# Cross-attention block: batch 0's second MLP product by seven block products, and the order of work around it

## The chip, the cores and the metric

The kernel runs on one core of a Trainium2 chip. A core has TensorE (matrix products into PSUM, with a separate weight load that runs beside them), VectorE, ScalarE and GpSimd (elementwise work), SyncE, whose queue (SP) issues most DMAs, and DMA engines. The metric is the device time of one execution in microseconds (us), the median of several runs. All data are float32; one matmul of this type leaves two records in the trace.

## The reference

Four batches; 512 rows of width 512; 16 heads of width 32; an inner width of 2048.

```python
x = layer_norm(hidden_states, ln1_w, ln1_b)
q, k, v = x @ q_w + q_b, enc @ k_w + k_b, enc @ v_w + v_b      # split into 16 heads
attn = softmax(where(mask, q @ k.T / sqrt(32), min))
hidden = (attn @ v) @ cproj_w + cproj_b + hidden_states
y = gelu(layer_norm(hidden, ln2_w, ln2_b) @ fc_w + fc_b)       # inner width 2048
return hidden + (y @ proj_w + proj_b)
```

## The kernel before

**Attention.** The work is cut into 16 units (4 batches x 4 groups of four heads) and each unit into two halves of 256 query rows: 32 blocks p = 0 to 31, written out one after the other. Every engine takes its instructions in the written order. A block begins with the attention product of an earlier half (`attend`, L401, tile `av`; from block 10 on that of half p-2), then computes eight score tiles (`scores`, L312), one in each of the eight PSUM banks. VectorE adds the mask and finds the minimum (`soften`, L319), ScalarE takes the exponential, VectorE transposes in 32x32 tiles into `tb` (`turn`, L331; the last transpose is L360). The blocks of `tb` are then exchanged between partition quarters into `pT`, `gt` or `xe` (`copies`, L385): four copies by GpSimd and twelve DMAs issued on SP. For half p into `pT` that can start only when the half before it in `pT` has been attended; from half 24 on `xe` takes turns with `pT`, and an exchange is issued at the end of its own block.

**Fills.** Other TensorE work is placed by hand between these steps: `put(p, ...)` (L1104) lists for block p the K, Q and V products of later units (`prep_k` L250, `prep_q` L260, `prep_v_pair` L288), the output product (`cproj` L451) and the next MLP items (`some(n)`, L1073). A block takes them in three places: fill(0) after the eighth score (not if the first item is an fc pair), fill(1) after the transposes, fill(2) at the end. The first two stop at a budget of one chain (`CHAIN`), and the exchange of the block is written between fill(1) and fill(2). Items of cost 0 are VectorE, GpSimd or DMA work.

**MLP in the blocks.** `products` (L571) lists in order what of batches 0 and 1 (`SPLIT`) runs in the blocks: fc pairs c (two columns of 128 of the inner width, seven products of half size, `fc_seven` L634) and proj quarters q (512 of the inner 2048). The activations of a quarter lie in `gT[q % 2]`, so the fc pairs of quarter q overwrite those of quarter q-2. A proj quarter is four items, one for each 128 rows: four 128x512 matmuls into one bank (`proj` L701), and one VectorE addition to the residual `hid`.

**Weights.** fc and proj weights go through a ring of eight entries of 256 KB in `pbt` (`load_mlp`, L582). The entry of a weight is reloaded, on SP and in list order, as soon as the item that uses it last (`last_use`) has been written. For the seven products of an fc pair GpSimd forms sums of its raw weights (`fc_sums`, L679), at the start of a block, for pairs at most two ahead of those computed:

```python
while count[3] < len(fc_pairs) and count[3] < count[4] + 2:
    b, c = fc_pairs[count[3]]
    if ("fcw", b, 2 * c + 1) not in S:
        return
```

Here `count[3]` counts pairs with sums, `count[4]` computed pairs. The weights of K and Q of a unit lie in `ptt`, two entries each, loaded two units ahead. After the blocks come the tail (rest of batch 1's first half of proj, `cproj` of batch 3) and `last_mlps` (L737), which the change touches only in where two tiles lie.

Of the kernel before, what the change touches and what calls it, by code (L numbers as in the profile page):

```python
# [35 lines left out]
IN_G = (1, 3, 5, 7)  # L36
IN_XE = (25, 27, 29, 31)

BY_ROW = ((1, 1), (1, 3))
# [12 lines left out]
def xattn_block(ctx: ExitStack, tc: tile.TileContext, x, rawT, encT, mask, q_w, k_w, v_w, c_w, fc_w, p_w, vecs, rows, out):  # L52
# [5 lines left out]

    const, keep, hids, tiles, small = pools(ctx, const=1, keep=1, hids=4, tiles=4, small=4)
    dram = ctx.enter_context(tc.tile_pool(name="dram", bufs=1, space=bass.MemoryType.DRAM))  # L60
# [28 lines left out]
    ys = const.tile([P, 3, 2, L // 2], F32, tag="ys", name="ys")  # L89
    wsum = const.tile([P, 2, 3, 2, P], F32, tag="wsum", name="wsum")  # L90

    def k_q(w, i):
# [117 lines left out]
    def load_rn(b):  # L210
        S["rows", b] = [hids.tile([P, L], F32, tag="hid2", bufs=2, name=f"rn_{b}_{i}") for i in range(2)]
        for i in range(2):
            nc.sync.dma_start(out=S["rows", b][i], in_=S["rn", b][i : i + 1, :].broadcast_to([P, L]))
# [26 lines left out]
    def load_w(w, queue=None, names=("wk", "wq", "wv")):  # L240
# [4 lines left out]
        for i, (n, src) in enumerate((("wk", k_w), ("wq", q_w), ("wv", v_w))):  # L245
            if n in names:
                S[n, w] = kqv_w(w, i)
                (queue or Q[0]).dma_start(out=S[n, w], in_=src[:, g, :, :])

    def prep_k(w):  # L250
        b, g = divmod(w, NG)
        kT = k_q(w, 0)
        acc = acc_tile(f"acck_{w}")
        for d in range(ND):
            nc.tensor.matmul(acc, S["wk", w][:, d, :], eT[:, d, :], start=(d == 0), stop=(d == ND - 1))  # L255
        load_w(w + 2, names=("wk",))
        nc.scalar.activation(kT, acc, AF.Identity, bias=vec[:, KB + g : KB + g + 1], scale=1.0)
        S["kT", w] = kT

    def prep_q(w):  # L260
        b, g = divmod(w, NG)
        qT = k_q(w, 1)
        parts = [slice(0, L)] if w else [slice(0, 2 * P), slice(2 * P, L)]
        for c in parts:
            acc = acc_tile(f"accq_{w}_{c.start}")[:, c]
            for d in range(ND):
                nc.tensor.matmul(acc, S["wq", w][:, d, :], xT[:, d, c], start=(d == 0), stop=(d == ND - 1))  # L267
            nc.scalar.activation(qT[:, c], acc, AF.Identity, bias=qb[:, g : g + 1], scale=-scale)
        load_w(w + 2, names=("wq",))
        S["qT", w] = qT  # L270
# [16 lines left out]

    def prep_v_pair(w):  # L288
        pair = range(w, w + 2)
# [13 lines left out]
        for u in pair:  # L303
            load_w(u + 2, names=("wv",))
            v_bias(u)

# [121 lines left out]
    def stays(b, t):  # L428

        return b == 0 or b == SPLIT and t < 2  # L430

    def load_h(b, *ts_):

        if ("xa", b) not in S:
            S["xa", b] = dram.tile([L, D], F32, tag=f"xa{b}", name=f"xa{b}")
        for t in ts_:
            if b == B - 1:

                S["h", b, t] = k_q(t // 2, t % 2)
            else:  # L440
                pool, tag, n = (tiles, "xn", 4) if not stays(b, t) else (hids, "hid2", 2) if b else (hids, "hid", 4)
                S["h", b, t] = pool.tile([P, D], F32, tag=tag, bufs=n, name=f"h_{b}_{t}")
# [93 lines left out]
    def load_hid(b, ts_):  # L536

        for t in ts_:
            if ("hid", b, t) not in S:
                S["hid", b, t] = hids.tile([P, D], F32, tag="hid", name=f"hid_{b}_{t}")  # L540
# [41 lines left out]
    def load_mlp():  # L582

        while count[0] < len(weights) and (count[0] < MW or weights[count[0] - MW][3] < count[1]):
# [4 lines left out]
            Q[0].dma_start(out=w, in_=fc_w[:, f, :, :] if name == "fc" else p_w[ts(f, P), :])  # L589
            S[name + "w", b, f] = w  # L590
            count[0] += 1
# [108 lines left out]

    def proj(b, q, t):  # L701
        gelus(q % 2)
        acc = acc_tile(f"accp_{b}_{q}_{t}")
        for k in range(FQ):
            nc.tensor.matmul(  # L705
                acc, gT[q % 2][:, k, ts(t, P)], S["pw", b, q * FQ + k], start=(k == 0), stop=(k == FQ - 1)
            )
        h = S["hid", b, t]
        nc.vector.tensor_tensor(h, acc, h, ALU.add)
        if q == NQ - 1:  # L710
            (nc.gpsimd if b == 0 else nc.sync).dma_start(out=out[b, ts(t, P), :], in_=h)
        count[1] += 1
        load_mlp()

# [22 lines left out]
    def last_mlps():  # L737
# [197 lines left out]
        for b, pairs, new in (  # L935
# [45 lines left out]
            if b == SPLIT:  # L981
                S["more"] = [hids.tile([P, D], F32, tag="hid2", bufs=2, name=f"more_{n}") for n in range(2)]
                S["more"] = [m.rearrange("p (c n) -> p c n", c=NP // 2) for m in (*S["more"], row[:, 2, :])]
                to_split.extend(w_sums(5, pt[:, 2]))
# [19 lines left out]

    def V(w):
        return [(CHAIN, lambda: prep_v_pair(w))]

# [65 lines left out]
    def some(n):  # L1073
# [5 lines left out]
        return taken  # L1079

    def hid_(b, *ts_):
        return do(lambda: load_hid(b, ts_))
# [21 lines left out]
    def put(p, *work, before=(), mid=()):  # L1104
# [52 lines left out]
    put(24, [q15], cb(2), V(14), do(lambda: y_sums(SPLIT)))  # L1157
    put(25, c[:3])
    put(26, c[3:], do(lambda: attend(12, 0)), some(2))
    put(27, some(3))  # L1160
    put(28, some(3))
    put(29, some(4))
    put(30, some(3), hid_(1, 2, 3))
    put(31, some(3))

    due = {p: (p - 2,) for p in range(10, 2 * NW)}
    due |= {p: (p - 3,) for p in range(3, 9)} | {9: (6,), 26: ()}
    for p in range(2 * NW):
# [6 lines left out]
        if p > 10:  # L1175
            fc_sums()

        def fill(n, work=fills[p]):
# [70 lines left out]
```

## Time and profile before

| | us |
|---|---|
| median of 3 runs | 762.18 (762.09 to 762.71) |
| profiled execution, time | 760.67 |
| its span, first to last instruction | 758.9 |
| TensorE busy | 753.9 |
| VectorE busy | 613.4 |
| ScalarE busy | 337.6 |
| GpSimd busy | 339.7 |

The blocks 11 to 31, which hold the MLP items, lie between 161.7 and 487.4 us of the span, the tail and the last MLPs after them. The granted TensorE clock was 0.999 of full speed. In the lines of the profile PE is TensorE, PEld its weight load, DVE VectorE, ACT ScalarE, POOL GpSimd, and SPq the issuing of DMAs by SyncE. A line of a timeline gives the start in us from the start of the span, the length in us, the engine, the line of the kernel, the operation, the tile written and the tiles read, and how many instructions are merged; in brackets stands the idle time just before it and what ended that. A line of a group gives the total busy time in us, the mean of one instruction in ns, and the idle time before. `hid`, `h` and `xa` are the residual rows, `wsum` the sums of fc weights, `pbt` holds the ring, `ptt` the K, Q and V weights and the exponentials.

### The profile page before, as it was taken

To read this page: it belongs to the slowest core of one execution; us is meant where nothing else is said; L and a number is where in the kernel's file an instruction comes from. 1 tells how busy PE (TensorE), PEld (TensorE's weight loads), DVE (VectorE), ACT (ScalarE), POOL (GpSimd) and SP (SyncE) were. 2 spreads that over 40 slices of the span, in tenths; PEclk is the share of its full clock that TensorE was granted. 3 is DMA by queue.
4 is the path that set the end of the run, shared out by engine and by line. 5 is a ranking of instruction groups with operands and counts; after the bars stand their busy time and mean duration, and the time that the engine had idled before them with its cause. 6 is when DMAs were issued, how large, how long until landed. Compare 5 with 4: busy or idle time off the path is not lost.

```text
span 758.9 us, 13040 instructions
## 1 busy us (share of the span) xinstructions
PE 753.9 (99%) x4418; PEld 517.8 (68%) x4418; DVE 613.4 (81%) x1222; ACT 337.6 (44%) x768; POOL 339.7 (45%) x352
## 2 busy tenths in 40 slices
PE   9999999999999999999999999999999999999998
PEld 6655555567574545475454566468888899988997
DVE  3889999879995777887887989949877986956865
ACT  2566766565873574647753567501302221022200
POOL 1549447368664873244575444432050004403153
PEclk9999999999999999999999999999999999999999
DMA  9989889467897776665756867776724402046001
GB/s 329 341 255 247 207 207 257 104 199 200 220 243 229 223 231 177 184 175 129 177 133 186 214 194 193 172 227 215 260 98 135 167 26 91 30 146 214 1 15 43
DMA packets 60577, 134.59 MB, mean 177 GB/s; under 512 B 11312, under 2 KB 17072, under 8 KB 60384
## 3 DMA queue, kind: packets, MB, share of 16 engines
q1 hardware_dynamic: 58448, 126.73, 58.4%
q0 software_dynamic: 1920, 7.01, 2.7%
q8 instruction: 35, 0.57, 0.3%
q14 instruction: 30, 0.25, 0.1%
q10 hardware_dynamic: 144, 0.02, 0.0%
HBM read 69.23 MB, written 11.02 MB: 106 GB/s over the span
## 4 chain that ended last, share of the span: by engine, by line
PE 99%; POOL 0%; issue 0%; DVE 0%; DVEq 0%; POOLq 0%
PE q L646 26%; PE accp L705 11%; PE r L792 10%; PE sc L317 8%; PE av L415 8%; PE acck L255 8%; PE accq L267 8%; PE accc L455 6%; PE accv L278 5%; PE accv L298 3%; PE q1p L853 2%; PE tp L166 1%; PE warm L1044 1%; PE q3p L835 0%; PE q5p L835 0%; PE q4p L835 0%
## 5 line engine op out<-in xcount | busy, mean ns | idle before, releaser
L327 ACT ACTIVATE ptt<-ptt,mn 128x512 f32<-128x512 f32 x256 | 181.7, 711 | 142.8 <-DVE mn L323 142.8
L323 DVE CUSTOM_DVE_ANT_0 ptt<-sc,mb 128x512 f32<-128x512 f32 x256 | 160.6, 682 | 19.9 <-PE sc L317 19.8
L335 DVE STREAM_TRANSPOSE tb<-ptt 128x1024 f32<-128x1024 f32 x128 | 153.3, 1217 | 0.0
L393 POOL COPY pT<-tb 32x1088 f32<-32x1088 f32 x96 | 104.5, 1089 | 83.5 <-DVE oT L420 34.6
L705 PE MATMUL accp<-pbt,gt 128*128 128x512 f32 x192 | 85.3, 596 | 0.0
L646 PE MATMUL q<-yT,gt 128*128 128x256 f32 x320 | 78.9, 379 | 0.0
L667 ACT ACTIVATE ga<-ga,vec 128x512 f32<-128x512 f32 x40 | 26.7, 714 | 93.3 <-DVE ga L600 93.3
L646 PEld LDWEIGHTS q<-yT,gt 128*128 128x128 f32 x320 | 60.8, 190 | 8.1
L705 PEld LDWEIGHTS accp<-pbt,gt 128*128 128x128 f32 x192 | 35.9, 190 | 44.6 <-issue 39.1
L317 PE MATMUL sc<-pbt 32*128 32x512 f32 x512 | 64.7, 614 | 0.0
L646 PE MATMUL q<-ys,gt 128*128 128x256 f32 x240 | 61.6, 379 | 0.0
L255 PE MATMUL acck<-xe,ptt 128*128 128x512 f32 x128 | 59.0, 604 | 0.0
L267 PE MATMUL accq<-xe,ptt 128*128 128x512 f32 (+1 forms) x136 | 58.4, 575 | 0.0
L646 PEld LDWEIGHTS q<-ys,gt 128*128 128x128 f32 x240 | 45.7, 190 | 6.1
L600 DVE TENSOR_TENSOR ga<-q,ga 128x512 f32<-128x512 f32 (+1 forms) x60 | 36.2, 603 | 16.3 <-PE q L646 13.5
L327 ACT ACTIVATION_READ_ACCUMULATOR ptt<-ptt,mn 128x1 f32 x256 | 47.8, 187 | 0.0
L415 PE MATMUL av<-pT,v 128*32 128x256 f32 x768 | 46.4, 382 | 0.0
L267 PEld LDWEIGHTS accq<-xe,ptt 128*128 128x128 f32 x136 | 24.9, 190 | 31.4 <-issue 22.8
L255 PEld LDWEIGHTS acck<-xe,ptt 128*128 128x128 f32 x128 | 23.8, 193 | 30.8 <-issue 24.0
L317 PEld LDWEIGHTS sc<-pbt 32*128 32x128 f32 x512 | 26.9, 184 | 24.8 <-issue 16.9
L455 PE MATMUL accc<-wc,oT 128*128 128x512 f32 x96 | 42.5, 598 | 0.0
L278 PEld LDWEIGHTS accv<-ptt,xe 128*128 128x128 f32 x320 | 37.0, 192 | 4.9 <-DVE mn L323 2.7
(231 smaller groups left out, 1270.4 us busy)
## 6 DMA issues: line engine op xcount, KB each, us to landing
pT<-tb SPq DMA_DIRECT2D x288, 136.0 KB, 2.4
pbt<-p_w_dram SPq DMA_DIRECT2D x40, 256.0 KB, 3.3
gt<-ws SPq DMA_DIRECT2D x20, 512.0 KB, 3.3
gt<-tb SPq DMA_DIRECT2D x48, 136.0 KB, 3.8
xe<-tb SPq DMA_DIRECT2D x48, 136.0 KB, 2.5
pbt<-fc_w_dram SPq DMA_DIRECT2D x24, 256.0 KB, 4.7
gt<-fc_w_dram SPq DMA_DIRECT2D x20, 256.0 KB, 3.3
ptt<-k_w_dram SPq DMA_DIRECT2D x16, 256.0 KB, 4.2
```

The lines of the kernel that those rows point to most:

```text
L255: nc.tensor.matmul(acc, S["wk", w][:, d, :], eT[:, d, :], start=(d == 0), stop=(d == ND - 1))
L267: nc.tensor.matmul(acc, S["wq", w][:, d, :], xT[:, d, c], start=(d == 0), stop=(d == ND - 1))
L317: nc.tensor.matmul(S["sc", w, qt][h], qT[r, ts(qt, P)], kT[r, :], start=True, stop=True)
L323: nc.vector.tensor_tensor_reduce(out=s, in0=S["sc", w, qt][h], in1=S["mb", w // NG], scale=1.0, scalar=FMAX, op0=ALU.add, op1=ALU.min, acc ...
L327: nc.scalar.activation(s, s, AF.Exp, bias=mn, scale=-1.0, accum_out=S["sums", w][:, qt, h : h + 1])
L335: nc.vector.transpose(tv[:, qt % 2, 2 * k : 2 * k + 2], S["ps", w, qt, k])
L393: nc.gpsimd.tensor_copy(pT[ts(i, HD), i], tb[ts(i, HD), i])
L415: nc.tensor.matmul(av[ts(h, HD), : 2 * P].rearrange(shape, **kw), v[:, t, ts(h, HD)], p[t][h], start=(t == 0), stop=(t == NT - 1),)
L455: nc.tensor.matmul(acc, S["oT", b][:, g, ts(t, P)], wc[:, g, :], start=(g == 0), stop=(g == NG - 1))
L646: nc.tensor.matmul(o, x[:, k], y[:, k], start=(k == 0), stop=(k == 1))
L705: nc.tensor.matmul(acc, gT[q % 2][:, k, ts(t, P)], S["pw", b, q * FQ + k], start=(k == 0), stop=(k == FQ - 1))
L792: nc.tensor.matmul(r, x[:, c], w[:, c], start=(c == 0), stop=(c == NP // 2 - 1))
```

## The change

Each proj quarter of batch 0 is computed by seven products of half size in each direction (x11 ... of activations and weights, with sums and differences on both sides) instead of eight. It becomes three items: part 0 (products q1, q5, q2), part 1 (q7, q6), part 2 (q3, q4). The sums that the first part needs (`proj_sums`, through `pre`) are formed by GpSimd ahead of it, the others by GpSimd in part 0, in place over activations and weights. ScalarE keeps q1 (and q5) in the place of blocks that are no longer needed; VectorE or GpSimd joins the results to the residual (`join`). Quarters in `FOUND1` and `FOUND5` join q1 and q5 directly from PSUM; in `COPIED` (quarter 3) ScalarE copies q3 and q4 and GpSimd joins them. Ring entries of the first two weights of a quarter are free after part 1, the others after part 2. K and Q weights have one entry each from unit 10 on, loaded one unit ahead, which frees the room for the two sum tiles x and y; quarter 3 takes the V weights' room. The fills of blocks 14, 15, 18 to 20, 22, 23 and 25 to 30 are laid out anew, with K and Q of unit 13 exchanged and K of unit 12 moved to block 19. The V biases of units 10 and 11 are held back to the start of the next block. The residual tiles of batches 0 and 1 become fixed tiles `hid4` and `hid2`.

```diff
+SINGLE = 10
+FOUND1, FOUND5, COPIED = ((0, 0),), ((0, 0), (0, 3)), ((0, 3),)
...
     def kqv_w(w, i):
-        n = 4 * i + 2 + w % 2
+        n = 4 * i + 2 + (w % 2 if i == 2 or w < SINGLE else 0)
...
+    def next_w(w, name):
+        if w != SINGLE - 1:
+            load_w(w + (2 if w < SINGLE else 1), names=(name,))
...
             load_w(u + 2, names=("wv",))
-            v_bias(u)
+            (held_back.append if later else run_)(lambda u=u: v_bias(u))
...
-    def pjs(b, q, *ts_):
-        return [("p", b, q, t) for t in ts_ or range(NT)]
+    def pjs(b, q, *parts):
+        return [("p", b, q, n) for n in parts or range(NT if b else 3)]
...
-    products += fcs(SPLIT, 0) + pjs(0, 3) + fcs(SPLIT, 1, 2, 3) + pjs(SPLIT, 0) + pjs(SPLIT, 1)
+    products += fcs(SPLIT, 0) + pjs(0, 3, 0) + fcs(SPLIT, 1) + pjs(0, 3, 1, 2) + fcs(SPLIT, 2)
+    products += fcs(SPLIT, 3) + pjs(SPLIT, 0) + pjs(SPLIT, 1)
...
-        last_use |= {(name, b, f): done - 1 for f in range(i * n, (i + 1) * n)}
+        n = range(i * n, (i + 1) * n)
+        if (name, b) == ("p", 0) and _[0] == 2:
+            n = n[2:]
+        last_use |= {(name, b, f): done - 1 for f in n}
...
+    def proj_blocks(b, q):
+        g = gT[q % 2]
+        w = [pbt[:, n * D : (n + 2) * D].rearrange("p (k f) -> p k f", k=2) for n in
+             (S.get(("pw", b, q * FQ + k), MW) for k in (0, 2))]
+        a11, a21, a12, a22 = (g[:, 2 * k : 2 * k + 2, ts(i, HL)] for k in range(2) for i in range(2))
+        w11, w12, w21, w22 = (w[k][:, :, ts(j, HL)] for k in range(2) for j in range(2))
+        x, y = (
+            ptt[:, n * D : (n + 1) * D].rearrange("p (k l) -> p k l", k=2)
+            for n in ((10, 11) if (b, q) == (0, NQ - 1) else (3, 7))
+        )
+        return a11, a21, a12, a22, w11, w12, w21, w22, x, y
+
+    def proj_sums(b, q, sides):
+
+        a11, a21, a12, a22, w11, w12, w21, w22, x, y = proj_blocks(b, q)
+        if "a" in sides:
+            gelus(q % 2)
+            add(nc.gpsimd, x, a21, a22)
+        if "w" in sides:
+            sub(y, w12, w11, nc.gpsimd)
+        if "a" in sides:
+            sub(a21, a11, a21, nc.gpsimd)
+        if "w" in sides:
+            sub(w12, w22, w12, nc.gpsimd)
...
+    def proj(b, q, part):
+
+        if b:
+            proj_whole(b, q, part)
+            return
+        a11, a21, a12, a22, w11, w12, w21, w22, x, y = proj_blocks(b, q)
+
+        def product(name, a, w):
+            o = acc_half(f"{name}_{b}_{q}")
+            for t in range(2):
+                for k in range(2):
+                    nc.tensor.matmul(o[:, t], a[:, k, ts(t, P)], w[:, k], start=(k == 0), stop=(k == 1))
+            return o
+
+        def join(engine, i, j, src):
+            h = hid4[:, 2 * i : 2 * i + 2, ts(j, HL)]
+            add(engine, h, src, h)
+
+        if part == 0:
+            q1 = product("q1j", a11, w11)
+            nc.scalar.copy(w11, q1)
+            if (b, q) in FOUND1:
+                join(nc.vector, 0, 0, q1)
+            q5 = product("q5j", x, y)
+            sub(x, x, a11, nc.gpsimd)
+            sub(y, w22, y, nc.gpsimd)
+            if (b, q) in FOUND5:
+                join(nc.vector, 0, 1, q5)
+                join(nc.vector, 1, 1, q5)
+            else:
+                nc.scalar.copy(a11, q5)
+            q2 = product("q2j", a12, w21)
+            join(nc.vector, 0, 0, q2)
+            sub(a12, a12, x, nc.gpsimd)
+            sub(w21, w21, y, nc.gpsimd)
+        elif part == 1:
+            q7 = product("q7j", a21, w12)
+            q6 = product("q6j", x, y)
+            add(nc.vector, y, q6, w11)
+            add(nc.vector, a21, q7, y)
+            late = () if (b, q) in FOUND1 else ((0, 0, w11),)
+            if (b, q) not in FOUND5:
+                late += (0, 1, a11), (1, 1, a11)
+            for i, j, src in late:
+                join(nc.gpsimd, i, j, src)
+        else:
+            q3 = product("q3j", a12, w22)
+            late = (1, 1, a21), (0, 1, y), (1, 0, a21)
+            if (b, q) in COPIED:
+                nc.scalar.copy(a12, q3)
+                late += (0, 1, a12), (1, 0, w22)
+            else:
+                join(nc.vector, 0, 1, q3)
+            q4 = product("q4j", a22, w21)
+            if (b, q) in COPIED:
+                nc.scalar.copy(w22, q4)
+            else:
+                join(nc.vector, 1, 0, q4)
+            for i, j, src in late:
+                join(nc.gpsimd, i, j, src)
+            if q == NQ - 1:
+                for t in range(NT):
+                    nc.gpsimd.dma_start(out=out[b, ts(t, P), :], in_=S["hid", b, t])
+        count[1] += 1
+        load_mlp()
...
-    put(14, [q], some(2), x1)
-    put(15, x2[:1], V(10), x2[1:2], do(lambda: load_raw(3)), some(2), do(lambda: store_rn(3)), some(1),
-        do(lambda: load_rn(3)), some(1))
+    put(14, [q], some(2), x1, pre(0, 0))
+    put(15, some(1), x2[:1], V(10, True), x2[1:2], do(lambda: load_raw(3)), some(2), do(lambda: (store_rn(3), load_rn(3))))
...
-    put(18, [q], some(2), [k])
+    put(18, [q], some(2), pre(0, 1))
+    k12 = k
     k, q, v = A(13)
-    put(19, some(2), [k])
-    put(20, [q], stat(1, 0, 1), some(2))
+    put(19, [k12], some(1), [q], stat(1, 0, 1))
+    put(20, [k], some(2))
...
-    put(22, [k, q], norm(1, 0, 1), some(2), norm(1, 2, 3))
+    put(22, [k, q], norm(1, 0, 1), some(2), norm(1, 2, 3), pre(0, 2))
     k15, q15, _ = A(15)
-    put(23, some(1), [k15], t2, pb_(1), some(1), h_(2, 2, 3, 0, 1))
+    put(23, some(1), [k15], t2, pb_(1), h_(2, 2, 3, 0, 1))
...
-    put(25, c[:3])
-    put(26, c[3:], do(lambda: attend(12, 0)), some(2))
-    put(27, some(3))
+    put(25, c[:3], pre(0, 3, "a"), some(1))
+    put(26, c[3:], do(lambda: attend(12, 0)), some(1))
+    put(27, some(3), mid=pre(0, 3, "w"))
     put(28, some(3))
-    put(29, some(4))
-    put(30, some(3), hid_(1, 2, 3))
+    put(29, some(3))
+    put(30, some(3), mid=hid_(1, 2, 3))
     put(31, some(3))
...
         if p > 10:
             fc_sums()
+        while held_back:
+            held_back.pop(0)()
```

More of the change, by code (lines that the diff above doesn't have):

```diff
@@ L57, in pools @@
         return [stack.enter_context(tc.tile_pool(name=n, bufs=k)) for n, k in bufs.items()]
-    const, keep, hids, tiles, small = pools(ctx, const=1, keep=1, hids=4, tiles=4, small=4)
+    const, keep, tiles, small = pools(ctx, const=1, keep=1, tiles=4, small=4)
     dram = ctx.enter_context(tc.tile_pool(name="dram", bufs=1, space=bass.MemoryType.DRAM))
@@ L90, in xattn_block @@
     wsum = const.tile([P, 2, 3, 2, P], F32, tag="wsum", name="wsum")
+    hid4 = const.tile([P, NT, D], F32, tag="hid4", name="hid4")
+    hid2 = const.tile([P, 2, D], F32, tag="hid2", name="hid2")
     def k_q(w, i):
@@ L210, in load_rn @@
     def load_rn(b):
-        S["rows", b] = [hids.tile([P, L], F32, tag="hid2", bufs=2, name=f"rn_{b}_{i}") for i in range(2)]
+        S["rows", b] = [hid2[:, i] for i in range(2)]
         for i in range(2):
@@ L286, in prep_v, with run_, prep_v_pair @@
             v_bias(w)
-    def prep_v_pair(w):
+    held_back = []
+    def run_(fn):
+        fn()
+    def prep_v_pair(w, later=False):
         pair = range(w, w + 2)
@@ L440, in load_h @@
             else:
-                pool, tag, n = (tiles, "xn", 4) if not stays(b, t) else (hids, "hid2", 2) if b else (hids, "hid", 4)
-                S["h", b, t] = pool.tile([P, D], F32, tag=tag, bufs=n, name=f"h_{b}_{t}")
+                S["h", b, t] = (
+                    (hid2 if b else hid4)[:, t] if stays(b, t)
+                    else tiles.tile([P, D], F32, tag="xn", name=f"h_{b}_{t}")
+                )
             Q[0].dma_start(out=S["h", b, t], in_=x[b, ts(t, P), :])
@@ L539, in load_hid @@
             if ("hid", b, t) not in S:
-                S["hid", b, t] = hids.tile([P, D], F32, tag="hid", name=f"hid_{b}_{t}")
+                S["hid", b, t] = hid4[:, t]
             Q[0].dma_start(out=S["hid", b, t], in_=S["xa", b][ts(t, P), :])
@@ L699, in fc_by_pair, with proj_whole @@
         load_mlp()
-    def proj(b, q, t):
+    def proj_blocks(b, q):
[7 more added lines that the diff above has]
+            for n in ((10, 11) if (b, q) == (0, NQ - 1) else (3, 7))
+        )
+        return a11, a21, a12, a22, w11, w12, w21, w22, x, y
[10 more added lines that the diff above has]
+            sub(w12, w22, w12, nc.gpsimd)
+    def proj_whole(b, q, t):
         gelus(q % 2)
@@ L704, in proj @@
         for k in range(FQ):
+            n = S["pw", b, q * FQ + k]
             nc.tensor.matmul(
-                acc, gT[q % 2][:, k, ts(t, P)], S["pw", b, q * FQ + k], start=(k == 0), stop=(k == FQ - 1)
+                acc, gT[q % 2][:, k, ts(t, P)], pbt[:, n * D : (n + 1) * D], start=(k == 0), stop=(k == FQ - 1)
             )
@@ L981, in last_mlps @@
             if b == SPLIT:
-                S["more"] = [hids.tile([P, D], F32, tag="hid2", bufs=2, name=f"more_{n}") for n in range(2)]
-                S["more"] = [m.rearrange("p (c n) -> p c n", c=NP // 2) for m in (*S["more"], row[:, 2, :])]
+                S["more"] = [
+                    m.rearrange("p (c n) -> p c n", c=NP // 2) for m in (hid2[:, 0], hid2[:, 1], row[:, 2, :])
+                ]
                 to_split.extend(w_sums(5, pt[:, 2]))
@@ L1003, in A, with V @@
         ]
-    def V(w):
-        return [(CHAIN, lambda: prep_v_pair(w))]
+    def V(w, later=False):
+        return [(CHAIN, lambda: prep_v_pair(w, later))]
     def C(b):
@@ L1079, in some, with pre @@
         return taken
+    def pre(b, q, sides="aw"):
+        return do(lambda: proj_sums(b, q, sides))
     def hid_(b, *ts_):
```

8 lines of the change are left out of this document (3 added, 5 removed).

## The prediction

> **What bounds the kernel now.** I read the page's busy times and its chain first, then the groups of instructions, then the timelines of TensorE, VectorE, GpSimd and the SP queue over the blocks.
>
> ```profile
> PE 753.9 (99%) x4418; PEld 517.8 (68%) x4418; DVE 613.4 (81%) x1222; ACT 337.6 (44%) x768; POOL 339.7 (45%) x352
> PE 99%; POOL 0%; issue 0%; DVE 0%; DVEq 0%; POOLq 0%
> ```
>
> TensorE is the chain from end to end. Its busy time is modelled, so I take its rate from the starts of successive groups (start, length, both in us):
>
> ```profile
> 228.08 13.90 PE L705 MATMUL accp<-pbt,gt 128*128 128x512 f32 x32
> 241.91 1.94 PE L415 MATMUL av<-pT,v 128*32 128x256 f32 x32
> ...
> 430.43 2.34 PE L317 MATMUL sc<-pbt 32*128 32x512 f32 x16
> 432.70 10.57 PE L705 MATMUL accp<-pbt,gt 128*128 128x512 f32 x24
> 443.19 1.93 PE L415 MATMUL av<-xe,v 128*32 128x256 f32 x32
> 445.06 2.00 PE L317 MATMUL sc<-pbt 32*128 32x512 f32 x16
> 446.99 1.99 PE L646 MATMUL q<-yT,pbt 128*128 128x256 f32 x8
> ...
> 453.13 1.89 PE L646 MATMUL q<-yT,pbt 128*128 128x256 f32 x8
> 454.86 1.03 PE L646 MATMUL q<-ys,wsum 128*128 128x256 f32 x4
> ```
>
> Groups follow each other without a hole. A 512-wide record takes (241.91 - 228.08)/32 = 432 ns, a 256-wide one (454.86 - 453.13)/8 = 216 ns, the attention products 1.87 us (443.19 to 445.06), the eight scores 1.93, an fc pair by seven products 6.14 (446.99 to 453.13). So a block with one fc pair and two new products takes 1.87 + 1.93 + 6.14 + 3.46 = 13.4 us of TensorE. One small wait shows: the scores at 430.43 took 0.34 us more than the 2.00 of the others. VectorE, at 81%, is the nearest other bound.
>
> **The gain.** Batch 0's proj issues 4 quarters x 16 matmuls, two records each: 128 records, 128 x 0.432 = 55.3 us; by the group's average below (85.3/192 = 444 ns) 56.9. I take 55.6, nearer the long run. The seven products are 4 x 28 matmuls, 224 records x 0.216 = 48.4 us. Gain 7.2 us (6.9 to 8.5), all on the chain.
>
> ```profile
> L705 PE MATMUL accp<-pbt,gt 128*128 128x512 f32 x192 | 85.3, 596 | 0.0
> L646 PEld LDWEIGHTS q<-yT,gt 128*128 128x128 f32 x320 | 60.8, 190 | 8.1
> ...
> L600 POOL TENSOR_TENSOR pbt<-wct,pbt 128x512 f32<-128x512 f32 x3 | 4.6, 1568 | 8.1 <-DVE wct L600 8.1
> ```
>
> **What is added, and its cover.** GpSimd's timeline in the blocks:
>
> ```profile
> 379.04 4.97 POOL L426 TENSOR_TENSOR h<-h,row 128x512 f32<-128x512 f32 x4
> ...
> 412.77 4.47 POOL L393 COPY pT<-tb 32x1088 f32<-32x1088 f32 x4 [2.37 <-PE accp L705]
> 428.19 0.72 POOL L600 TENSOR_TENSOR wsum<-pbt 128x256 f32<-128x256 f32 x1 [10.95 <-DMA pbt<-fc_w_dram]
> ...
> 431.16 4.47 POOL L393 COPY xe<-tb 32x1088 f32<-32x1088 f32 x4
> ```
>
> VectorE loses 16 PSUM additions and gets 8, 5, 5 and 5 in the four quarters: 7 more of about 0.66 us, 4.6 us over 17 blocks. ScalarE gets 8 copies; it is 44% busy. GpSimd gets 32 sums and 21 joins of 128x512. Its addition of that size takes 1.24 us in the blocks (4.97/4) and 1.57 in the last stage (its group above); I take 1.25, the nearer place: 53 x 1.25 = 66 us, 45% to 54%. Those sums are free only where nothing waits for GpSimd. Through block 24 I find room: the first sums of a quarter are issued a block ahead, the attention copies they delay by about 1 us (4.47 us a block, needed a block later) have some 5 us of slack. The tightest place is block 15, where the store of the LayerNorm rows and their reload now follow each other behind the last product:
>
> ```profile
> 235.98 1.30 SPq L206 DMA_DIRECT2D rn<-rnT  x4
> 240.42 0.82 SPq L213 DMA_DIRECT2D rn<-rn  x2
> ...
> 244.41 7.91 SPq L398 DMA_DIRECT2D pT<-tb  x12
> ...
> 412.70 8.94 SPq L398 DMA_DIRECT2D pT<-tb  x12
> ...
> 442.25 8.15 SPq L398 DMA_DIRECT2D pT<-tb  x12
> 450.50 1.03 SPq L589 DMA_DIRECT2D pbt<-fc_w_dram  x2
> ```
>
> SP waits 3.1 us between the end of the store (237.28) and the reload (240.42). In the changed order the exchange of pair 15 stands behind that wait, so its 7.9 us of issue begin some 3.7 us after the block's start and land just as block 17's attention wants them: 0 to 1 us, taken as 0. Freeing the K and Q weight entry for the next unit only, exchanging K and Q of unit 13, and moving unit 12's K one block later issue the same loads and matmuls, each at least half a block before its use: 0. The two V biases held back join GpSimd's longest queue (block 16, ten 128x512 operations): its copies come about 1.5 us later, inside their slack: 0.
>
> **Where the cover goes: blocks 27 to 31.** Here GpSimd stands between weights and TensorE. The rows needed, VectorE over block 29, and the landings of ring loads in 415 to 470 us and of the exchanges (median us):
>
> ```profile
> 445.25 0.42 DVE L420 TENSOR_TENSOR oT<-av,xe 128x256 f32<-128x256 f32 x1 [1.26 <-PE av L415]
> 446.22 0.69 DVE L323 CUSTOM_DVE_ANT_0 ptt<-sc,mb 128x512 f32<-128x512 f32 x1 [0.54 <-PE sc L317]
> ...
> 455.73 0.41 DVE L360 STREAM_TRANSPOSE tb<-rr 128x256 f32<-128x256 f32 x1
> 456.06 0.66 DVE L600 TENSOR_TENSOR gt<-q,p 128x512 f32<-128x512 f32 x1
> 456.82 1.95 DVE L600 TENSOR_TENSOR gt<-q,gt 128x512 f32<-128x512 f32 x3
> ```
>
> ```profile
> DMA to landing us min/median/max: 2.6/4.2/5.0
> ```
>
> ```profile
> pT<-tb SPq DMA_DIRECT2D x288, 136.0 KB, 2.4
> ```
>
> A block whose first fill is an fc pair ends its transposes 11.1 us after its scores start (456.14 - 445.06), then spends 2.7 us on the pair's additions (456.06 to 458.77).
>
> (a) Block 27: y of quarter 3 (GpSimd, in the middle of the block) must be ready for q5. Count from the end of q4 in block 26. GpSimd: VectorE is still at its transposes and joins q3 and q4 (2.7), the last late join 1.25, copies of pair 26 4.5, four weight sums of fc pair (1,1) 3.0 (428.19 to 431.16), y 1.25: 12.7. TensorE: 1.87 + 1.93 + 6.14 + q1 1.73 = 11.7. Wait 1.0; by 1.57 per GpSimd sum 1.6, with 1 us less on either chain 0. I take 1.0.
>
> (b) Block 28 ends with the two part-1 additions behind the fc additions: after 11.1 come 2.7 + 1.3 + the attention output 0.42 + the first score 0.61 = 16.1 us, where TensorE wants that score's bank at 13.4 + 1.93 = 15.3. Wait 0.8 (0 to 1.2).
>
> (c) Block 29 is the main cost. fc (1,1) now runs in block 28, so at the start of block 29 the planner's rule (sums at most two pairs ahead) lets GpSimd take the sums of fc pair (1,3); in the kernel before it came there a block later. Its raw weights are loaded when part 1 has freed w11 and w12, and on SP that load stands behind pair 28's exchange. From the end of block 28's transposes: exchange 8.2, second load issued 0.5 later, landing 4.2, four sums 3.0, and only then the late joins; three of them, 3.75, read a21, which lies in the rows of gT[1] that fc (1,2) of the same block overwrites. That is 19.6 us. VectorE stands at its first addition of fc (1,2) one block later, 13.4 + 0.8 = 14.2. It waits 5.4, with the softmax of block 30 behind it; TensorE has four products' banks and some 0.4 us in hand, so it loses about 5.0 (3 to 7 by landings of 2.6 to 5.0, exchanges of 7.9 to 8.9 and joins of 1.57). The row at 428.19 shows such a wait already, 10.95 us, but with only copies behind it.
>
> (d) Block 31. SP must load the next proj weights before pair 29's exchange, and the first goes over w22, which the fifth late join still reads. From the third join: two joins 2.5, six loads at 0.5, exchange 8.2, landing 2.4: 16.1. TensorE: fc additions, attention output and first score on VectorE 3.7, fc (1,3) 6.1, one proj part 3.5: 13.3. Wait 2.8 (1 to 4.5).
>
> **Sum.** -7.2 for the products, -0.3 for the small wait at 430.43, which the longer ones swallow, +1.0 + 0.8 + 5.0 + 2.8: +2.1 us. The profiled execution took 760.67 us (span 758.9), 1.5 below the median of 762.18; 760.67 + 2.1 = 762.8, and at the median 764.3.
>
> **Rivals.** (1) GpSimd and SP keep up: weights for (1,3) land early enough or the joins come before the sums, and only (a) and (b), at most 2 us, remain: 762.18 - 7.2 - 0.3 + 0 to 2 = 754.7 to 756.7. For it: TensorE is 99% and every cover up to block 24 holds. Against it: GpSimd takes its queue in the written order, and the exchange's issue time has been 7.9 to 8.9 us in every block. It decides if the chain of (c) is shorter than 14.5 us instead of 19.6. (2) Half of it: (c) at its lower end, (d) gone with it: 762.18 - 7.5 + 1.8 + 3 = 759.5. (3) The change costs more: the reload in block 15 takes its 1 us, joins run at 1.57, (c) and (d) at their upper ends: 762.18 - 7.5 + 1 + 1.6 + 1.2 + 7 + 4.5 = 770.0. (4) The narrower products don't pay, because a stationary load of 190 ns (above) shows beside each: 96 more loads are 18.2 us, time 762.18 + 18.2 - 7.2 = 773.2. Against it: 216 ns a record in the fc groups, with a load for each, leaves no room for an exposed 190.
>
> [...]
>
> **How the numbers follow.** The forecast case has 0.53 and 762 to 768 as its own range; rival 1 0.23, rival 2 0.16, rival 3 0.07, rival 4 0.01. Leaving out the better part of rival 1 and the far ends of 3 and 4 gives 756.5 to 769. A change of 0.2%, 1.5 us, is about what a measurement here can tell: under 760.7 lie rival 1 and most of rival 2 (0.33); within it the rest of rival 2 and the lower end of the forecast (0.14); above 763.7 0.53.
>
> **What would show it.** The batch-0 proj groups as 8-record groups 1.73 us apart (gain). In block 29, GpSimd's first wsum waiting for a landing of fc weights, and VectorE's first addition to gt waiting for a GpSimd join to hid4, with the next scores stretched by about 5 us (c). The first ring load after quarter 3 waiting for GpSimd and the attention products of block 31 starting late (d). A wait before q5 of quarter 3 in block 27 (a). I am wrong if TensorE's groups run on without holes through blocks 27 to 31; then the time is near 755.

## The result, and the profile after

The changed kernel took 769.41 us (median of 4 runs, 768.14 to 771.1), beside 762.13 for the kernel before on the same chip: ratio 1.0103, 95% interval 1.007 to 1.0135. It is 1% slower. The forecast was 764.3 with a range to 769.0: the direction was right, the size 5.1 us short, and the time lies 0.4 us outside the range. The profiled execution took 771.1 us (span 769.3), 10.4 more than that of before. Of these, 2.5 us arose before block 15, which every comparison below leaves out: its scores start at 219.14 us before and at 221.65 after, while in a second execution of the same changed kernel (below) they start at 219.36.

The page of the changed kernel, busy times and chain:

```profile
PE 756.9 (98%) x4514; PEld 538.6 (70%) x4514; DVE 618.1 (80%) x1229; ACT 341.3 (44%) x776; POOL 406.2 (53%) x405
PE 92%; DMA 3%; POOL 2%; DVE 2%; issue 1%; SPq 1%; ACT 1%; DVEq 0%; POOLq 0%
```

TensorE's busy time has grown by 3 us although it does 7 us less work, and the chain, once TensorE alone, now passes through DMA, GpSimd and VectorE. First the part that went as meant, TensorE in block 15 (start and length in us):

```profile
221.65 2.00 PE L330 MATMUL sc<-pbt 32*128 32x512 f32 x16
...
235.77 1.89 PE L769 MATMUL q7j<-pbt,gt 128*128 128x256 f32 x8
...
240.95 1.89 PE L769 MATMUL q4j<-pbt,gt 128*128 128x256 f32 x8
```

A product comes every 1.73 us (three from 235.77 to 240.95), 216 ns a record. Now TensorE over blocks 26 to 31:

```profile
401.96 2.70 PE L330 MATMUL sc<-pbt 32*128 32x512 f32 x16
...
426.20 1.99 PE L769 MATMUL q5j<-ptt 128*128 128x256 f32 x8 [0.64 <-POOL ptt L616]
...
445.20 3.04 PE L330 MATMUL sc<-pbt 32*128 32x512 f32 x16
...
459.73 1.14 PE L330 MATMUL sc<-pbt 32*128 32x512 f32 x8
461.69 1.12 PE L330 MATMUL sc<-pbt 32*128 32x512 f32 x2 [0.81 <-DVE gt L619]
463.03 2.15 PE L330 MATMUL sc<-pbt 32*128 32x512 f32 x6 [0.23 <-DVE gt L619]
465.12 3.17 PE L665 MATMUL q<-yT,pbt 128*128 128x256 f32 x8
468.08 1.58 PE L665 MATMUL q<-ys,wsum 128*128 128x256 f32 x4
...
472.95 3.60 PE L750 MATMUL accp<-pbt,gt 128*128 128x512 f32 x8
481.06 3.64 PE L428 MATMUL av<-xe,v 128*32 128x256 f32 x32 [4.51 <-DMA xe<-tb]
484.63 2.78 PE L330 MATMUL sc<-pbt 32*128 32x512 f32 x16
...
497.84 1.93 PE L428 MATMUL av<-pT,v 128*32 128x256 f32 x32
```

The four holes stand where the prediction put them: before q5 (a), at the scores of block 29 (b), inside the scores of block 30 (c), before the attention products of block 31 (d). Behind (c) and (d) TensorE does not only wait, it also runs slower: the eight records at 465.12 take 2.96 us instead of 1.73, the attention products 3.57 instead of 1.87, the scores 2.71 instead of 1.93. What ends the waits of (c) and (d), on GpSimd, VectorE and the SP queue:

```profile
454.18 0.73 POOL L619 TENSOR_TENSOR wsum<-pbt 128x256 f32<-128x256 f32 x1 [5.43 <-DMA pbt<-fc_w_dram]
...
462.09 1.26 POOL L619 TENSOR_TENSOR hid<-pbt,hid 128x512 f32<-128x512 f32 x1
```

```profile
460.94 0.69 DVE L619 TENSOR_TENSOR gt<-q,p 128x512 f32<-128x512 f32 x1 [4.05 <-POOL hid L619]
```

```profile
442.93 7.49 SPq L411 DMA_DIRECT2D pT<-tb  x12
...
463.38 2.92 SPq L608 DMA_DIRECT2D pbt<-p_w_dram  x6
466.40 12.50 SPq L411 DMA_DIRECT2D xe<-tb  x12
```

GpSimd stands 5.43 us at the weight sums of fc pair (1,3), until the raw weights issued behind pair 28's exchange land; the five late joins come after, from 457.17 to 463.35, and VectorE's addition waits 4.05 us for the third. The proj loads leave SP when the fifth join has ended (463.35), and pair 29's exchange behind them takes 12.50 us to issue, where that of pair 28 took 7.49.

From the start of block 15's scores to the start of the last attention product above, the kernel before takes 487.37 - 219.14 = 268.23 us, by the starts of its two rows

```profile
219.14 2.00 PE L317 MATMUL sc<-pbt 32*128 32x512 f32 x16
...
487.37 1.93 PE L415 MATMUL av<-pT,v 128*32 128x256 f32 x32
```

and the changed one 497.84 - 221.65 = 276.19: 7.96 more. Taken from the starts of groups (the idle times in brackets go by modelled ends, and come out a little shorter), the waits seen in it are (a) 0.8, (b) 1.05, (c) 3.46, the slow fc pair behind it 1.7, (d) 4.6, the slow attention products and scores behind it 2.5, and in the scores of blocks 18 and 26 0.4 and 0.7: 15.2 us. The rest, 7.96 - 15.2 = -7.2, is what the products saved. The second execution gives the same remainder: it took 493.92 - 219.36 = 274.56 us for this stretch, 6.33 more than the kernel before, and its waits and slow groups, taken in the same way, add up to 13.5.

### The profile page after: what moved, and what is told of

It reads as the page before. It is cut to its first block, busy times and chain, and to the rows that moved or that the text cites. A ratio compares the mean times of both kernels' runs of the same rounds, so it can differ in the third digit from the quotient of the medians.

```text
span 769.3 us, 13328 instructions
## 1 busy us (share of the span) xinstructions
PE 756.9 (98%) x4514; PEld 538.6 (70%) x4514; DVE 618.1 (80%) x1229; ACT 341.3 (44%) x776; POOL 406.2 (53%) x405
## 4 chain that ended last, share of the span: by engine, by line
PE 92%; DMA 3%; POOL 2%; DVE 2%; issue 1%; SPq 1%; ACT 1%; DVEq 0%; POOLq 0%
PE q L665 23%; PE r L893 10%; PE sc L330 8%; PE av L428 8%; PE acck L263 7%; PE accq L275 7%; PE accc L470 5%; PE accv L286 5%; PE accp L750 3%; PE accv L311 3%; PE q1p L954 2%; PE tp L170 1%; DMA pbt<-p_w_dram 1%; PE q5j L769 1%; PE q7j L769 1%; PE q2j L769 1%
## 5 line engine op out<-in xcount | busy, mean ns | idle before, releaser
L330 PE MATMUL sc<-pbt 32*128 32x512 f32 x512 | 70.9, 622 | 1.0 <-DVE gt L619 1.0
L330 PEld LDWEIGHTS sc<-pbt 32*128 32x128 f32 x512 | 28.7, 187 | 30.2 <-issue 17.9
L439 POOL TENSOR_TENSOR hid<-hid,row 128x512 f32<-128x512 f32 x18 | 23.9, 1357 | 45.4 <-DMA hid<-xa 45.4
L322 POOL TENSOR_TENSOR v<-v,row 128x512 f32<-128x512 f32 x16 | 20.3, 1278 | 41.0 <-ACT v L291 33.7
```

The lines of the kernel that those rows point to most:

```text
L330: nc.tensor.matmul(S["sc", w, qt][h], qT[r, ts(qt, P)], kT[r, :], start=True, stop=True)
```

## The experiments

Each kernel is the changed kernel with the edit shown. Ratios are to the kernel before, run on the same chip (761.3 to 761.8 us); its executions spread over several us, so a median alone tells no more than some 1.5 us, and the traces decide what happened.

**Weight sums a block later.**

```diff
-        if p > 10:
+        if p > 10 and p != 29:
             fc_sums()
```

> Changed kernel, but GpSimd takes the weight sums of fc pair (1,3) at the start of block 30, as in the kernel before, and not at the start of block 29. Theory (order): in block 29 the late joins of quarter 3 no longer stand behind weights that land late, so the stretched scores of block 30 (5.4 us instead of 1.9), the wait of block 31's attention products (4.5 us) and the records at a low clock after both (some 4 us) go: 769.4 - 12 = 757.4 us. Rival (load): GpSimd, with 66 us more work, is simply too slow in these blocks, whatever its order: within 2 us of 769. Rival (half): only the scores of block 30 are cured and the exchange of pair 29 stays late: 764.

764.35 us (ratio 1.0034, 1.0015 to 1.0053). TensorE in blocks 30 and 31:

```profile
457.04 2.00 PE L330 MATMUL sc<-pbt 32*128 32x512 f32 x16
...
464.55 2.08 PE L665 MATMUL q<-ys,wsum 128*128 128x256 f32 x4 [3.58 <-POOL wsum L616]
...
475.51 1.93 PE L428 MATMUL av<-xe,v 128*32 128x256 f32 x32
```

The scores of block 30 take 2.00, so the wait of (c) is gone, and the place of the sums ahead of the joins was its cause. The attention products of block 31 start without a wait, but (d) is only hidden: the exchange of pair 29 still took 11.03 us (458.68 to 469.71) and, with some 2.4 us of landing, ended near 472.1, and TensorE, held up by a new wait, came at 475.51. For the sums now come too late for their own pair: 3.58 us of waiting, and slow records behind (the four that the row begins with take 2.08 by its modelled end, 1.03 elsewhere). About 5 us came back, not the 12 that (c) and (d) cost, because this wait took their place.

**Ring entries freed as before.**

```diff
-        if (name, b) == ("p", 0) and _[0] == 2:
-            n = n[2:]
```

> Changed kernel, but all four ring entries of a proj quarter are freed after its last part, as they were before the change. Theory (order): the weights of fc pair (1,3) are then asked for only in block 29, so that the planner leaves their sums to block 30 and the joins run at once: about 758 us, like the kernel with the sums moved by hand. Rival (load): the later weights make every block tighter, 770 or more.

762.94 us (1.002, 1.0003 to 1.0038). With the entries free only after part 2, the raw weights of (1,3) are loaded too late to be known at the start of block 29, and the sums move to block 30 of themselves. The time is 5 us above the 758 that was expected, for the reason of the first experiment, whose waits this trace repeats:

```profile
464.93 2.08 PE L663 MATMUL q<-ys,wsum 128*128 128x256 f32 x4 [3.60 <-POOL wsum L614]
```

So freeing the entries a part sooner, meant to bring the loads forward, is what let GpSimd begin the sums a block too soon.

**Quarter 3's last products joined by VectorE.**

```diff
-FOUND1, FOUND5, COPIED = ((0, 0),), ((0, 0), (0, 3)), ((0, 3),)
+FOUND1, FOUND5, COPIED = ((0, 0),), ((0, 0), (0, 3)), ()
```

> Changed kernel, but VectorE joins q3 and q4 of quarter 3 from PSUM, so that no ring entry waits for GpSimd's last joins. Theory (two separate waits): SP can load the next proj weights and start pair 29's exchange at once, so the 4.5 us wait of block 31 and the 2.5 us of low clock after it go; the stretched scores of block 30 stay: 762.4 us. Rival (one cause): both waits hang on the third join alone and nothing changes, 769. Rival (all gone): 757.

761.99 us (1.0003, 0.9984 to 1.0021). (d) goes and (c) stays, as (d)'s theory says: w22 is no longer read by a join of GpSimd, and the exchange starts 1.4 us before the scores of block 30 (455.51 against 456.86), where in the changed kernel it starts 6.7 us after them (466.40 against 459.73).

```profile
458.80 1.12 PE L330 MATMUL sc<-pbt 32*128 32x512 f32 x2 [0.80 <-DVE gt L619]
...
462.23 1.99 PE L665 MATMUL q<-yT,pbt 128*128 128x256 f32 x8
...
471.90 1.93 PE L428 MATMUL av<-xe,v 128*32 128x256 f32 x32
```

Here the fc pair behind the same holes of (c) runs at full speed (granted clock 1.00 in every window from 460 to 470 us), which it did not in the changed kernel.

**Quarter 3 as before, quarters 0 to 2 by seven.** `proj` sends quarter 3 to `proj_whole`, which stores the finished rows, `last_use` keeps its four entries, quarter 3 has no sums ahead, and the fills of blocks 27 to 29 are those of before:

```diff
-products += fcs(SPLIT, 0) + pjs(0, 3, 0) + fcs(SPLIT, 1) + pjs(0, 3, 1, 2) + fcs(SPLIT, 2)
-products += fcs(SPLIT, 3) + pjs(SPLIT, 0) + pjs(SPLIT, 1)
+products += fcs(SPLIT, 0) + pjs(0, 3) + fcs(SPLIT, 1, 2, 3) + pjs(SPLIT, 0) + pjs(SPLIT, 1)
...
-        if b:
+        if b or q == 3:
```

> Quarters 0 to 2 by seven products as in the changed kernel, quarter 3 as before the change (four whole items, VectorE additions, the fills of blocks 27 to 29 as before). Theory (order): the three quarters keep their gain of 3 x 1.8 = 5.4 us less about 1.1 us of short waits in blocks 18 and 26, and nothing of blocks 27 to 31 is lost: 757.9 us. Rival (load): sums and joins beside the attention don't pay anywhere, 762 or more.

758.14 us (0.9948, 0.993 to 0.9965): faster than both kernels. The cover holds for three quarters, but for the 0.7 us in the scores of block 26, which are there too; the loss lies in the fourth.

**TensorE kept busy during the wait of (d).**

```diff
+        if p == 31:
+            busy = acc_tile("busy")
+            for _ in range(40):
+                nc.tensor.matmul(busy[:, :P], ident, ident, start=True, stop=True)
         for pair in due.get(p, ()):
```

> The changed kernel with 40 products of the identity (128x128, nothing reads them, some 4.3 us) between the proj part and the attention products of block 31, where TensorE stood idle for 4.5 us and then ran 5.6 us at a granted clock of 0.50. Theory (the idleness itself lowers the clock): the attention products still wait for the exchange of pair 29, but they and the scores behind them take 1.9 and 1.9 us as elsewhere instead of 3.6 and 2.8: 2.5 us less than the changed kernel's 769.4, 767. Rival (the clock falls with the transfers, which fill the DMA engines there): the clock stays at 0.50 and the time at 769.4. If the products only come on top of the wait: 773.

772.34 us (1.0121, 1.0092 to 1.0151). The 40 products were twice as long as estimated, since each is two records:

```profile
474.65 9.09 PE L1281 MATMUL busy<-ident 128*128 128x128 f32 x80
483.67 1.93 PE L428 MATMUL av<-xe,v 128*32 128x256 f32 x32
```

They outlast the wait, so the time says nothing; but the rows behind them are at full speed (1.87 us from the attention products to the scores). The windows of this kernel (TensorE busy, weight loads, VectorE, ScalarE, GpSimd, then granted clock, DMA share and GB/s) speak against the transfers as the cause:

```profile
475.00:480.00 5.00, 5.00 (x47) 5.00 (x46) 0.54 (x1) 0.00 (x0) 0.91 (x1) 1.00 0.92 244
```

The DMA engines are 0.92 busy and the clock stays at 1.00. In the changed kernel itself they are 0.99 to 1.15 busy from 470 to 475 us, with TensorE busy and the clock at 1.00.

**The same, with 18 products,** and **the changed kernel once more** beside it (no edit).

```diff
-            for _ in range(40):
+            for _ in range(18):
```

> The run that keeps TensorE busy, with 18 products of the identity instead of 40: those came as two records each and took 9.0 us, 5 longer than the wait, so their gain was hidden. 18 are 36 records of 113 ns, 4.1 us, about the wait of 4.5. Theory (idleness lowers the clock, the transfers do not): clock 1.00 in block 31, attention products 1.9 and scores 1.9, and 2.5 us less than the changed kernel run beside it: ratio of the two 0.997. Rival (the clock falls with the transfers): no difference. If the products delay what they stand before: 1 to 2 us more than the changed kernel.

> The changed kernel once more, unaltered, as the measure for the run beside it and for what varies from execution to execution. Theory: the waits of (a) to (d) come back at the same places and lengths (0.7, 1.1, 3.5, 4.5 us), since they follow from the order of the queues; how long the granted clock stays low after them may differ (after the wait of block 30 it was low for 3.4 us in one execution, not at all in another), so the time may differ by 2 to 3 us. 768 to 771. Rival (the first measurement fell badly): 764 to 766, some of the waits smaller.

766.36 us (1.0062, 1.0042 to 1.0081) against 769.6 (1.0104, 1.008 to 1.0127): 3.2 us less for adding work that nobody reads; the two intervals just meet, so the rows have to show it. TensorE, first with the 18 products in block 31, then the changed kernel in blocks 29 to 31:

```profile
473.51 4.18 PE L1281 MATMUL busy<-ident 128*128 128x128 f32 x36
478.10 1.93 PE L428 MATMUL av<-xe,v 128*32 128x256 f32 x32 [0.40 <-issue]
479.96 2.00 PE L330 MATMUL sc<-pbt 32*128 32x512 f32 x16
```

```profile
442.58 3.04 PE L330 MATMUL sc<-pbt 32*128 32x512 f32 x16
...
460.39 3.10 PE L330 MATMUL sc<-pbt 32*128 32x512 f32 x6 [0.23 <-DVE gt L619]
463.43 3.78 PE L665 MATMUL q<-yT,pbt 128*128 128x256 f32 x8
...
477.95 3.62 PE L428 MATMUL av<-xe,v 128*32 128x256 f32 x32 [2.64 <-DMA xe<-tb]
```

With the 18 products the clock stayed at 1.00 here (475 to 485 us), and the attention products and scores of block 31 took 3.8 us together; in the two profiles of the changed kernel they took 6.3 and 5.5. So 1.7 to 2.5 us are shown at the place itself, where 2.5 had been expected; the rest of the 3.2 is within what varies.

The ratio of the changed kernel came back (1.0104 after 1.0103), and so did the waits (a) to (c); (d) came out at 2.64, not the 4.5 that was expected. The reason is in the rows: TensorE ran slowly for longer behind (c) (6.8 us at a clock of 0.50 instead of 3.4), so it reached block 31 later, and the exchange, which does not wait for it there, landed at almost the same point. From the scores of block 29 to the attention products of block 31 it is 481.06 - 445.20 = 35.9 us in the first profile of the changed kernel and 477.95 - 442.58 = 35.4 in the second. What TensorE loses to its clock behind (c) is thus paid out of the wait of (d), while what it loses behind (d) comes on top.

**Weight sums behind the joins of the same block.** With the first edit, and

```diff
             if q == NQ - 1:
+                fc_sums()
                 for t in range(NT):
                     nc.gpsimd.dma_start(out=out[b, ts(t, P), :], in_=S["hid", b, t])
```

> The changed kernel with the weight sums of fc pair (1,3) taken on GpSimd behind the five late joins of quarter 3 in block 29, neither ahead of them (as changed) nor a block later (the first experiment, 764.4). Theory (only GpSimd's order costs in blocks 29 to 31): the joins end near 456, the sums near 459, before fc (1,3) of block 30 wants them at 461; the proj loads follow the fifth join at 456 and the exchange ends by 468, before block 31. No wait of (c) or (d) is left, only (a) 0.8 and (b) 1.1 and the small ones: 769.4 less 5.2 and 7.0 and the 1 us that goes with them: 756.5 to 757.5. Rival (the late landing of the raw weights or ScalarE's copies keep a wait alive): 760 or more, with fc (1,3) waiting for its sums.

762.57 us (1.0006, 0.9983 to 1.003). The scores of block 30 and fc (1,3) run without a hole, so (c) is gone and no new wait stands in its place; (d) stays, and this was not expected: the time is the rival's, but by another wait than the rival's. TensorE and SP:

```profile
458.47 2.00 PE L330 MATMUL sc<-pbt 32*128 32x512 f32 x16
...
473.70 3.43 PE L428 MATMUL av<-xe,v 128*32 128x256 f32 x32 [3.55 <-DMA hid<-xa]
```

```profile
457.05 2.87 SPq L608 DMA_DIRECT2D pbt<-p_w_dram  x6
460.01 10.98 SPq L411 DMA_DIRECT2D xe<-tb  x12
```

The profile names the load that was issued right behind the exchange; the exchange itself ended at 470.99, 2.7 us ahead of the products. With TensorE on time, a fifth join that ends at 457 is still too late: 2.9 us of loads, 11.0 of exchange and 2.7 of landing end at 473.7, and TensorE is there at 470.1. (c) and (d) are two waits, each able to show without the other.

**The first and the third together.**

> The first and the third experiment together: sums of fc pair (1,3) a block later, and quarter 3's last two products joined by VectorE (COPIED empty). Theory: without the two joins that wait for ScalarE, GpSimd gets to its copies some 5 us earlier and to the sums before fc (1,3) wants them: the wait of 3.6 us and the slow clock behind it, which the first experiment showed, go: 757. Rival (the sums are late whatever the joins do, because copies stand before them): a wait of 1 to 3 us at fc (1,3) and 760.

762.04 us (0.9993, 0.9973 to 1.0012). The rival was right about the wait, and 2 us low in the time: GpSimd's third join waits 4.91 us for VectorE's join to the same rows, the copies of pair 29 follow, and the sums are late for their pair again.

```profile
466.64 2.08 PE L665 MATMUL q<-ys,wsum 128*128 128x256 f32 x4 [2.22 <-POOL wsum L616]
```

**Sums behind the joins, VectorE's joins, and y first.** The `fc_sums` of the kernel with the sums behind the joins, `COPIED = ()`, and

```diff
-    put(27, some(3), mid=pre(0, 3, "w"))
+    put(27, some(3), before=pre(0, 3, "w"))
```

> The sums of fc pair (1,3) behind the late joins, quarter 3's last products joined by VectorE, and the weight side of quarter 3's sums at the start of block 27, ahead of the weight sums of fc pair (1,1), instead of in its middle. Theory: the waits of (a), (c) and (d) are all gone and only (b) stays: the kernel before less 7.2 plus 1.1 plus about 1 for the small ones: 762.1 - 5.1 = 757 or a little less, 0.5 to 1 us under the run with the sums in the middle alone. Rival ((a) does not go, since the sums move the wait to fc (1,1) in block 28): the same as that run.

756.09 us (0.9914, 0.9887 to 0.9941), the best of all and 13 us under the changed kernel, with all of its products. TensorE at q5 (no idle time before it), block 30 and block 31:

```profile
422.67 1.89 PE L769 MATMUL q5j<-ptt 128*128 128x256 f32 x8
...
456.10 2.49 PE L330 MATMUL sc<-pbt 32*128 32x512 f32 x16
...
468.19 1.93 PE L428 MATMUL av<-xe,v 128*32 128x256 f32 x32
```

The waits of (a), (c) and (d) are gone, and no slow clock is left (1.00 in every window from 440 to 490 us); (b), the 0.7 us in the scores of block 26 and 0.5 us in those of block 30 remain.

## Why the prediction was right or wrong

- **The gain** was right: -7.2 us is what the sums over blocks 15 to 31 leave for it, in both profiles, where -7.2 and -0.3 had been put. Rival 4 falls with it: the new groups run at 216 ns a record with 190 ns loads beside them.
- **Cover through block 24, priced at 0**: 0.4 us in block 18, in one of the two profiles of the changed kernel (the other has 2.00 there). Block 15 is smooth, exchange included. Behind block 24, the scores of block 26 took 2.70 in every kernel that computes quarter 2 by seven products: 0.7 us that no step had. VectorE's rows there show the order of (b), one quarter earlier: it makes quarter 2's two part-1 additions at 402.06 and 402.79 and comes to the first score only at 403.40. In the kernel before, which has no such additions, these scores took 2.04. No run takes the additions away, so this cause is read from the rows and not tested.
- **(a)** 1.0 predicted, 0.8 measured, at the place and by the engine named. In the last kernel it is gone, and of its three edits only the move of y ahead of the weight sums acts before that place; in the runs with one of the other two the row of q5 kept its 0.65 us of idle time.
- **(b)** 0.8 predicted, 1.05 measured. No run removes it alone.
- **(c)** 5.0 predicted. The mechanism is shown by the runs that move the sums. The third join ended 18.0 us after the start of pair 28's exchange (442.93 to 460.94) instead of 19.6, since the exchange took 7.5 and not 8.2 and the weights landed sooner, so the wait itself was 3.46. That (c) with its slow clock comes to 5.2, near the 5.0, is luck: a shorter wait and a term that the prediction did not have.
- **(d)** 2.8 (1 to 4.5) predicted, and this is the step that failed. The mechanism was right, one term of it was mis-sized: "exchange 8.2" measured 12.5. From the third join to the attention products it took 20.1 us (2.4 to the loads, 3.0 for them, 12.5, and 2.2 for the landing), not 16.1; TensorE was there after 15.5, not 13.3, 1.7 of that by its slow clock behind (c), and so the wait was 4.6. This exchange stands right behind six loads of 256 KB and beside four stores of 256 KB. The prediction took its figure from rows of 7.91 to 8.94 us and held that the issue had been 7.9 to 8.9 us in every block. That is misread: several took 7.50, and in block 15 the SP queue of the kernel before has the longest one, right behind six loads of 256 KB and with no store beside it until 227.70 us:

```profile
214.87 2.83 SPq L589 DMA_DIRECT2D pbt<-fc_w_dram  x2
217.81 1.79 SPq L184 DMA_DIRECT2D xn<-x_dram  x4
219.79 12.12 SPq L398 DMA_DIRECT2D pT<-tb  x12
```

At this place the exchange took 12.1 us here and 11.1 in the changed kernel. The chain of waits of the changed kernel shows what pair 29's exchange hung on:

```profile
465.86 9.97 DMA pbt<-p_w_dram
...
478.30 2.45 DMA xe<-tb
```

The last of the six loads took 9.97 us to land, and the ninth of the twelve exchange DMAs was issued on that landing. SP did not stand all the while: its list of waits puts 3.2 of the 12.5 us down to landings of these loads, and single issues took up to 1.9 us where the shortest took 0.5. Without loads right ahead of it pair 28's took 7.49 in the changed kernel; with the six, pair 29's took 9.95 (VectorE's joins) to 12.5. No run separates the loads from the stores. The landing, 2.45, was as predicted.

- **The sum** had no term for the clock, which is the other half of what failed. TensorE ran at a granted clock of 0.50 for a while after these waits, and this added 1.7 us behind (c) and 2.5 behind (d) in the first profile. In windows of 1 us of the changed kernel (the last three columns are granted clock, DMA share and GB/s):

```profile
465.00:466.00 1.00, 1.00 (x5) 0.75 (x5) 1.00 (x5) 1.00 (x4) 1.00 (x2) 0.89 0.75 287
466.00:467.00 1.00, 1.00 (x4) 0.82 (x3) 1.00 (x5) 1.00 (x5) 0.96 (x2) 0.50 1.01 395
...
469.00:470.00 1.00, 1.00 (x6) 0.90 (x5) 1.00 (x2) 0.00 (x0) 0.96 (x1) 0.91 1.04 342
...
479.00:480.00 1.00, 0.00 (x0) 0.00 (x0) 0.00 (x0) 0.00 (x0) 0.00 (x0) 0.71 1.00 226
...
486.00:487.00 1.00, 1.00 (x12) 0.20 (x4) 0.42 (x1) 0.00 (x0) 0.96 (x2) 0.87 0.90 231
```

Between the edges it is 0.50 throughout, so from the shares at the edges the low clock lasts from 465.8 to 469.2 (3.4 us) and from 479.4 to 486.3 (6.8 us). The mean over the whole span, 0.993, hides it. Keeping TensorE busy through the wait of (d) kept the clock at 1.00 there, in both runs that did it.

Together: by the first profile (c) and (d) with their clock cost 12.2 us where 7.8 stood, 4.4 more, and blocks 18 and 26 add up to 1.1; the other differences are 0.3 us or less. 764.3 + 4.4 + 1.1 = 769.8. By the second it is 11.0 and 0.7: 764.3 + 3.2 + 0.7 = 768.2. The medians measured are 769.4 and 769.6.

Of the rivals, (1), GpSimd and SP keep up with 754.7 to 756.7, is what the last kernel reaches at 756.09 by a changed order. (2), half of it, did not happen as the change was written. (3), 770.0, is nearest in time, by other terms: it had the joins at 1.57 us, which took 1.27, and the reload of block 15, which cost nothing; only its upper end of (d), 4.5, came true.

## What to carry to other kernels

Where engines run their queues in the written order, look at what a faster or earlier step lets through: here an entry freed a part sooner let GpSimd start, and then stand in (5.43 us), sums that nobody needed yet, in front of joins that were wanted. In this kernel a wait on TensorE had to be priced with the slow clock behind it (1.7 us behind (c) and 2.5 behind (d) in the first profile, none behind (c) with VectorE's joins), and the twelve exchange DMAs with the loads and stores around them (12.5 us), not with their issue time elsewhere (7.5). Taking one cause away at a time showed waits that stood behind each other, and only the run that reordered them all, with quarter 3 by seven products as well, had nearly the whole gain (756.09 against 758.14 with quarter 3 as before).

## What the runs showed of the hardware

In these runs idleness, not load, halved the granted clock of TensorE: 0.50 in the wait of 4.5 us and behind it, and 1.00 with 0.92 of the DMA engines busy when identity products filled that wait. Six waits of 2.2 to 4.5 us, before sums of fc (1,3) or before block 31, left TensorE with nothing to do, and in all six its records were slow behind the wait; the windows of five of them show the clock falling, 2.1 to 3.2 us after its last product ended. In the windows of nine traces between 440 and 490 us the low clock lasted 3.4 us five times and 6.8 us four times, and no other time was seen: 3.4 where TensorE was at work again within some 0.35 us of the fall, 6.8 where it still stood for some 0.7 us or more, or had only the held-up scores of block 30 to do. The same two holes of 0.8 and 0.2 us in block 30, with TensorE standing or half used for some 3 us around them, were followed by a full clock in one kernel (VectorE's joins), by 3.4 us at 0.50 in two executions and by 6.8 us in two; why they differ was not settled, and no run shows why the clock stays low for these two lengths.

The issue of twelve exchange DMAs on SP took 7.5 us for pair 28 in the changed kernel, 10 to 12.5 for pair 29 behind six loads and beside four stores of 256 KB each, and 12.1 right behind six loads in block 15 of the kernel before: in these runs it is no fixed cost of the queue.
